# A sandwich of retention and feed-forward: the flag of an early branch, and the last block's closing steps

## The chip, the cores and the metric

The kernel runs on one core of a Trainium2 chip. The metric is the device time of one execution in microseconds (us); a run's result is the median of several executions. Beside these times there is one execution taken by the hardware profiler, from which the page, its views and the trace come.

## The reference, cut to what matters

x has 4 sequences of 1024 tokens with 512 features, in f32. Two residual layers follow each other, each between two layer norms:

```python
x = x + _layernorm(_L0_attn_ref(_layernorm(x), Wq, Wv, Wo, Wg, gamma, lnb, beta))
x = x + _layernorm(_L0_ffn_ref(_layernorm(x), gate_w, up_w, down_w, gate_s, up_s, down_s))
```

The first is a retention: q and v are projected, v runs through a decaying scan along the tokens, the product with q is normalised, gated by silu(x @ Wg.T) and projected by Wo. The second is a feed-forward layer of 1536 hidden units, silu(gate) * up and then down. Its three weights go through float8_e4m3fn before they are used. For weights beyond the range of that format the kernel has a second program, described below.

## The kernel before, in words

**Blocks.** The 4096 tokens are worked in 8 blocks of 512 (`NB` = 8, `TB` = 512), each in 4 tiles of 128 tokens (`NS` = 4). The main loop (line 1214) runs over blocks t; within a block it runs over 12 steps i (`NI` = 12), one for each 128 of the hidden units. A step multiplies gate and up for these units (8 matmuls of 128x512 each), fuses them, and adds an earlier step's product into the four sums of down (2 matmuls for each of the 4 tiles). Between these stands the retention of block t + 1 (`b`), the start of block t + 2 (`n`), and the closing norm of block t - 1 (`l`). Blocks 6 and 7 have fewer such guests, and block 7 (the last, `f.last`) has no retention beside it.

**Order.** The order of the work is written out by hand. Every operation goes through the helper at line 67 (`InOrder`), which keeps it in program order on its engine; that is why nearly all rows of the profile name line 75. All DMAs of the middle of the kernel are issued by SyncE (SP), in this one order too, so a DMA that waits holds those behind it. The weights of the retention come through a ring of four buffers (`w_ring`, `fetch_weights`, line 429): a pass of TensorE that is done releases the load that is four passes ahead.

**Step and lag.** In step i, `fuse(i)` (line 935) takes up's sum times its scale times the gate on VectorE (DVE), ScalarE (ACT) casts it into the upper half of a pair, and `rest(i)` (line 946) forms the lower half on DVE. `down(i)` (line 953) multiplies both halves. It is put `lag` steps behind (line 918): 2 in most blocks, 4 in the last, which has room for seven pairs.

**The tail.** Behind the loop `lag` + 1 steps of down are left (line 1495). They are ordered by tile, so that tile 0's sum closes first: all steps of tile 0 but the last and two of tile 1, then tile 0's last step, then the rest of tile 1, then tiles 2 and 3. Then, for each tile s, DVE multiplies by the scale of down (`scale`) and takes the statistics, ACT takes the root of the variance, DVE adds tile s - 1 to its residual and SP stores it, DVE takes the reciprocal, and the tile is normed: by ACT (`shift_scale`, line 238) for tiles 0 to 2, by DVE (`center_scale`, line 235) for tile 3. Tile 3 is added in two halves (`add_halves`, line 1015); SP stores the first half and ACT the second.

**Flag and branch.** While the weights are rounded, each piece leaves in `over` what tells whether it held a value beyond the format. `pass_over` (line 200) turns that into one number in three parts: DVE sums it and SP writes it as a column to DRAM; SP reads the column back as a row; DVE takes its maximum and SP writes it to DRAM as `flag`. The parts run in steps 2, 3 and 4 of block 7 (line 1373). Behind the last matmul of the program's order, every engine loads `flag` into a register (line 1508), gives a branch hint (line 1514) and later reaches the branch (line 1569). If the flag is zero, it is taken to a short closing piece of code, behind the code of the second program, which rounds the weights exactly and does everything again. There SP waits for its eight DMA semaphores in turn, and then all engines meet at a barrier (line 1615).

Of the kernel before, what the change touches and what calls it, by code (L numbers as in the profile page):

```python
# [15 lines left out]
ALU = mybir.AluOpType  # L16

P = 128
# [5 lines left out]
def sandwich(  # L24
# [20 lines left out]
    nc = tc.nc  # L45
# [4 lines left out]
    TB = 512  # L50
    NS = TB // P
    NB = NT // TB
# [14 lines left out]
    class InOrder:  # L67


        def __init__(self, engine):  # L70
            self.engine = engine
# [5 lines left out]
    pe, dve, act, pool, sp = (  # L77
        InOrder(e) for e in (nc.tensor, nc.vector, nc.scalar, nc.gpsimd, nc.sync)
    )
# [116 lines left out]
    def rounds(n):  # L196
        for _ in range(n):
            next(rounding, None)
# [710 lines left out]
    class Ffn:  # L909
# [3 lines left out]
        def __init__(self, a):  # L913
            self.t, self.kept = a.t, a.kept
            self.parts = [a.x1nT[:, 0], a.x1nT[:, 1]]
            self.f, self.g = {}, {}
            self.last = self.t == NB - 1
            self.lag = 4 if self.last else 2
            self.x1, self.d = [], [None] * NS
            if self.last:  # L920
                self.more = [
                    big.tile([P, 2, 2, TB], F32R, tag=tag, name=f"more_{tag}") for tag in ("xnT", "y")
                ]
# [83 lines left out]
            center(self.d[s], self.d[s], self.mv[:, s, :])  # L1007

        def add(self, s, engine=pool):
            if engine is dve and s == NS - 1:  # L1010
                return self.add_halves(s)
            engine.tensor_tensor(self.d[s], self.d[s], self.x1[s], ALU.add)
            self.store(s)

        def add_halves(self, s):
            for h, queue in enumerate((sp, act)):
                cols = ts(h, D // 2)
                dve.tensor_tensor(self.d[s][:, cols], self.d[s][:, cols], self.x1[s][:, cols], ALU.add)
                queue.dma_start(out[ds(self.t * TB + s * P, P), cols], self.d[s][:, cols])

        def store(self, s):
            sp.dma_start(out[ds(self.t * TB + s * P, P), :], self.d[s])
# [24 lines left out]
    early, later = slice(0, TB // Q // 2), slice(TB // Q // 2, TB // Q)  # L1047
# [162 lines left out]
    splitter.store(7)  # L1210
    rounds(3)

    l = None
    for t in range(NB):
        f, n = Ffn(a), None
        fast = b is not None and b.fast
        for i in range(NI):
# [104 lines left out]
            if t == 0 and i == 9:  # L1322
                load = b.move_x1n(2)
# [10 lines left out]
            if fast and i == 9:  # L1334
                b.o_moments(2)
                loads = [b.move_x1n(s) for s in range(2)]
# [32 lines left out]
            if fast and i == 7:  # L1369
                b.rest_of_y()  # L1370
            splitter.at(t, i, "mid")
            if t == NB - 1 and 1 < i < 5:
                next(passing, None)
            if n and t and i == 2:
                l.fetch(0, 2)
# [115 lines left out]
        l, a, b = f, b, n  # L1491
# [11 lines left out]
    for s in range(2, NS):  # L1503
        for i in steps:
            l.down(i, [s])
    beyond = None
    if flag is not None:
        loads, (beyond,) = nc.values_load_multi_w_load_instructions(
            flag, min_val=0, max_val=0x7F800000,
            skip_runtime_bounds_check_because="it is compared with zero alone",  # L1510
        )
        for load in loads:
            tc.keep_in_program_order(load)
        tc.mark_branch_hint_location("beyond", beyond, engines=mybir.ALL_ENGINES)
    for s in range(NS):
        l.scale(s)
        l.stats(s)
        l.root(s)
        if s:
            l.add(s - 1, dve)  # L1520
        l.inverse(s)
        l.norm(s, shift_scale if s < NS - 1 else center_scale)
    l.add(NS - 1, dve)
    return beyond


# [33 lines left out]
@with_exitstack  # L1560
def retention_ffn_sandwich(ctx: ExitStack, tc: tile.TileContext, *args):


    nc = tc.nc
    out, seq = args[-2:]
    kept = ctx.enter_context(tc.tile_pool(name="flag", bufs=1, space=bass.MemoryType.DRAM))
    flag = kept.tile([1, 1], I32, tag="flag", name="flag")
    beyond = sandwich(tc, *args, flag=flag)
    with tc.If(beyond == 0, preferred_fallthrough_block=False, label="beyond") as within:
        pass  # L1570
    with within.Else():
        with tc.tile_pool(name="rounded", bufs=1, space=bass.MemoryType.DRAM) as kept_rounded:
            weights = round_exactly(tc, kept_rounded, args[8:11], ("gate_w8", "up_w8", "down_w8"))
            sandwich(tc, *args[:8], *weights, *args[11:])
# [44 lines left out]
```

## Time and profile before

| what | us |
|---|---|
| median of three runs (904.69 to 905.27) | 905.08 |
| the profiled execution | 904.03 |
| its span, from the first to the last instruction | 902.2 |
| TensorE busy in the span | 881.1 (98%) |
| DVE busy | 629.8 (70%) |
| ACT busy | 419.0 (46%) |
| POOL busy | 238.9 (26%) |
| mean granted TensorE clock | 0.997 |
| DMA of code: q8, 33 packets | 0.54 MB |
| DMA of code: q14, 37 packets | 0.30 MB |

PE stands for TensorE's matmuls, PEld for its weight loads, POOL for GpSimd. A small q behind an engine's name (SPq, ACTq) means its queue of instructions that are not counted as busy, such as issues of DMAs, branches and waits. In a row of a timeline come the start, the duration, the engine, the line, the operation, what it writes and reads, and in brackets how long the engine had been idle before and what ended that. Rows of equal instructions are merged ("x8"). `pd` are the sums of down, `pfg` and `pfu` those of gate and up, `d` the last norm's tiles, `mvd` their mean and variance, `fuse`, `more_xnT` and `more_y` the pairs. In the rows of a source line come the durations of its instructions (least, median and most, in ns) and the start of the first and last. The page's DMA queues q8 and q14 have the kind "instruction": they load code, in packets of 16 KB (q8) and 8 KB (q14). The end of the span, 1.83 us before the end of the execution's time, is the barrier.

### The profile page before, as it was taken

The numbers are of one execution on the slowest core, as the hardware profiler recorded it, in microseconds if no ns is written. First come the engines' busy times: TensorE is split into PE (matmuls) and PEld (weight loads), VectorE is DVE, ScalarE is ACT, GpSimd is POOL, SyncE is SP. The second block draws the span as 40 slices with busy tenths as digits, with TensorE's granted clock in tenths as the row PEclk, the third lists the DMA queues.
The fourth block names the chain that finished last, engine by engine and source line by source line (L and its number), as shares of the span: only waits on it lengthen the run. The fifth ranks groups of instructions, "written<-read, shape, count | busy, mean of one in ns | idle before, by whom it ended". The sixth has DMA issues, their size and how long they took to land. (4 is left out here: it accounts for less than half of the span.)

```text
span 902.2 us, 12010 instructions
## 1 busy us (share of the span) xinstructions
PE 881.1 (98%) x3948; PEld 738.6 (82%) x3948; DVE 629.8 (70%) x1071; ACT 419.0 (46%) x741; POOL 238.9 (26%) x304
## 2 busy tenths in 40 slices
PE   9999999889999999999999999999999999999995
PEld 7465777678888888888888888888888888888885
DVE  4898788677587766876668675876758756665545
ACT  1358566533645336453464435553364523644323
POOL 1215212201415024230423214141232403322020
PEclk9999999999999999999999999999999999999998
DMA  9974444767563674646754766728746565424021
GB/s 284 304 217 157 151 171 157 205 234 237 171 176 96 232 237 136 153 153 204 250 149 97 232 205 193 187 58 258 226 148 152 154 197 149 152 73 117 0 94 50
DMA packets 116154, 153.73 MB, mean 170 GB/s; under 512 B 10931, under 2 KB 54708, under 8 KB 116020
## 3 DMA queue, kind: packets, MB, share of 16 engines
q1 hardware_dynamic: 115220, 152.23, 55.1%
q8 instruction: 33, 0.54, 0.2%
q10 hardware_dynamic: 864, 0.66, 0.2%
q14 instruction: 37, 0.30, 0.1%
HBM read 117.98 MB, written 39.06 MB: 174 GB/s over the span
## 5 line engine op out<-in xcount | busy, mean ns | idle before, releaser
L75 PE MATMUL pfg<-x1nT,gate_sb 128*128 128x512 f32 x768 | 182.8, 381 | 3.3 <-ACT gate L75 3.2
L75 PE MATMUL pfu<-x1nT,up_sb 128*128 128x512 f32 x768 | 183.2, 381 | 0.8 <-DVE gate L75 0.8
L75 PE MATMUL pd<-down_sb,fuse 128*128 128x512 f32 x720 | 170.5, 379 | 0.0
L75 PEld LDWEIGHTS pfg<-x1nT,gate_sb 128*128 128x128 f32 x768 | 144.2, 189 | 26.7 <-ACT gate L75 6.2
L75 PEld LDWEIGHTS pfu<-x1nT,up_sb 128*128 128x128 f32 x768 | 145.0, 189 | 23.6 <-issue 1.7
L75 PEld LDWEIGHTS pd<-down_sb,fuse 128*128 128x128 f32 x720 | 141.4, 197 | 14.5
L75 DVE SCALAR_TENSOR_TENSOR gate<-pfu,us_sb,gate 128x512 f32<-128x512 f32 x96 | 71.8, 747 | 67.0 <-PE pfu L75 54.8
L75 ACT CAST fuse<-gate 128x512 fp32r<-128x512 f32 x90 | 55.6, 617 | 126.9 <-DVE gate L75 125.2
L75 ACT ACTIVATE gate<-pfg,gs_sb 128x512 f32<-128x512 f32 x96 | 65.6, 683 | 95.5 <-PE pfg L75 95.4
L75 POOL TENSOR_SCALAR mv<-mv 128x1 f32<-128x1 f32 (+1 forms) x82 | 22.8, 278 | 315.0 <-DVE mv L75 312.9
L75 DVE TENSOR_TENSOR fuse<-gate,fuse 128x512 fp32r<-128x512 f32 x90 | 71.7, 797 | 7.4 <-ACT fuse L75 7.3
L75 POOL TENSOR_TENSOR d<-d,x 128x512 f32<-128x512 f32 x28 | 41.7, 1510 | 84.5 <-ACT d L75 70.6
L75 DVE BATCH_NORM_STATS2 st<-x 128x6 f32<-128x512 f32 x64 | 43.6, 681 | 15.2 <-POOL x L75 12.5
L75 POOL TENSOR_TENSOR mv<-mv,nhalf 128x1 f32<-128x1 f32 (+1 forms) x75 | 51.8, 691 | 6.2
L75 POOL TENSOR_TENSOR x<-x,x1n 128x512 f32<-128x512 f32 x32 | 44.7, 1403 | 23.4 <-ACT x1n L75 15.0
L75 ACT ACTIVATE pv<-pv 128x512 f32<-128x512 f32 x28 | 16.3, 581 | 52.9 <-PE pv L75 52.9
L75 POOL TENSOR_TENSOR sqsum<-sqsum,sq 128x512 f32<-128x512 f32 x24 | 33.6, 1401 | 16.0 <-ACT sq L75 8.7
L75 POOL TENSOR_TENSOR ysum<-y 128x512 f32<-128x512 f32 x8 | 10.2, 1275 | 104.2 <-DVE y L75 104.2
L75 DVE TENSOR_TENSOR y<-pq,y 128x512 f32<-128x512 f32 x28 | 19.1, 682 | 22.5 <-PE pq L75 22.5
L75 DVE SCALAR_TENSOR_TENSOR y<-y,lnb_sb,mids 128x512 f32<-128x512 f32 x28 | 27.0, 965 | 7.1 <-ACT mids L75 7.0
L75 ACT ACT_TABLE_LOAD x19 | 24.4, 1283 | 15.5 <-DVE var L75 11.1
L75 DVE BATCH_NORM_STATS2 st<-po 128x6 f32<-128x512 f32 x32 | 21.9, 683 | 13.4 <-PE po L75 13.4
(222 smaller groups left out, 1482.8 us busy)
## 6 DMA issues: line engine op xcount, KB each, us to landing
x<-in_x SPq DMA_DIRECT2D x52, 256.0 KB, 5.6
kept<-x SPq DMA_DIRECT2D x32, 256.0 KB, 2.9
x<-kept SPq DMA_DIRECT2D x32, 256.0 KB, 4.4
out<-d SPq DMA_DIRECT2D x31, 256.0 KB, 2.0
w_ring<-dtop_v SPq DMA_DIRECT2D x24, 256.0 KB, 4.1
w_ring<-dlow_v SPq DMA_DIRECT2D x24, 256.0 KB, 3.2
w_ring<-ddiff_v SPq DMA_DIRECT2D x24, 256.0 KB, 3.6
w_ring<-dtop_q SPq DMA_DIRECT2D x24, 256.0 KB, 2.6
```

The source lines that it names most:

```text
L75: return lambda *args, **kwargs: tc.keep_in_program_order(op(*args, **kwargs))
```

## The change

Four things change. `pass_over` runs in steps 0, 1 and 2 of block 3. ACT, SP and POOL load the flag and give their hint in step 5 of block 6; they load it once more at the old place, for the branch, without a hint. DVE and PE load and hint at the old place. The last block's lag becomes 5. And the last tile is centred by DVE (`center`) behind the add of tile 2 and ahead of the reciprocal, in place of `center_scale` behind it; its two halves are then multiplied by the reciprocal root and added to the residual in one operation each (`spread`).

```diff
-            self.lag = 4 if self.last else 2
+            self.lag = 5 if self.last else 2
...
-            if engine is dve and s == NS - 1:
-                return self.add_halves(s)
...
-        def add_halves(self, s):
+        def center(self, s):
+            dve.tensor_scalar(self.d[s], self.d[s], self.mv[:, s, 0:1], None, ALU.subtract)
+
+        def spread(self, s):
+
             for h, queue in enumerate((sp, act)):
                 cols = ts(h, D // 2)
-                dve.tensor_tensor(self.d[s][:, cols], self.d[s][:, cols], self.x1[s][:, cols], ALU.add)
-                queue.dma_start(out[ds(self.t * TB + s * P, P), cols], self.d[s][:, cols])
+                d = self.d[s][:, cols]
+                dve.scalar_tensor_tensor(
+                    d, d, self.mv[:, s, 1:2], self.x1[s][:, cols], ALU.mult, ALU.add
+                )
+                queue.dma_start(out[ds(self.t * TB + s * P, P), cols], d)
...
+    late = [mybir.EngineType.DVE, mybir.EngineType.PE]
+    early = [mybir.EngineType.Activation, mybir.EngineType.SP, mybir.EngineType.Pool]
+
+    def load_flag(engines):
+        loads, (value,) = nc.values_load_multi_w_load_instructions(
+            flag, engines, min_val=0, max_val=0x7F800000,
+            skip_runtime_bounds_check_because="it is compared with zero alone",
+        )
+        for load in loads:
+            tc.keep_in_program_order(load)
+        return value
+
+    def hint(value, engines):
+
+        tc.mark_branch_hint_location("beyond", value, engines=engines)
...
-            if t == NB - 1 and 1 < i < 5:
+            if flag is not None and t == NB - 2 and i == 5:
+                hint(load_flag(early), early)
+            if t == 3 and i < 3:
                 next(passing, None)
...
-        tc.mark_branch_hint_location("beyond", beyond, engines=mybir.ALL_ENGINES)
+        hint(beyond, late)
+    final = NS - 1
     for s in range(NS):
         l.scale(s)
         l.stats(s)
         l.root(s)
         if s:
             l.add(s - 1, dve)
+        if s == final:
+            l.center(s)
         l.inverse(s)
-        l.norm(s, shift_scale if s < NS - 1 else center_scale)
-    l.add(NS - 1, dve)
+        if s < final:
+            l.norm(s, shift_scale)
+    l.spread(final)
     return beyond
```

## The prediction, as put on record before the changed kernel was run

> **What bounds the kernel now.** I read the page's shares first, then busy time by stretch, then the chain that ended last, and last the end of the run by engine. The page puts PE at 98% of a 902.2 us span, and in the stretches 434 to 540 and 828 to 892.7 us it is busy for 105.98 of 106.00 and 64.59 of 64.70 us. No matmul goes away here, so up to 892.65 us (the last matmul row below, 891.62 + 1.03) the change can only lose time. What can be won lies in the 9.5 us behind it. The chain view shows who holds that stretch (start, duration, what):
>
> ```profile
> 893.73 0.60 DVE d L75
> ...
> 894.36 0.70 DVE st L75
> ...
> 895.97 0.56 DVE d L75
> ...
> 896.89 0.42 DVE d L75
> ```
>
> DVE's chain ends at 897.31, with 4.9 us of span still to come. The timelines of PE and DVE tell why DVE ends so late (start, duration, work, idle before it in brackets):
>
> ```profile
> 882.12 1.89 PE L75 MATMUL pfu<-x1nT,up_sb 128*128 128x512 f32 x8
> ...
> 886.44 0.59 PE L75 MATMUL pd<-down_sb,more_xnT 128*128 128x512 f32 x2
> ...
> 891.62 1.03 PE L75 MATMUL pd<-down_sb,more_xnT 128*128 128x512 f32 x4
> ```
>
> ```profile
> 887.13 0.69 DVE L75 TENSOR_TENSOR d<-pd,ds_sb 128x512 f32<-128x512 f32 x1 [0.87 <-PE pd L75]
> ...
> 889.24 0.69 DVE L75 TENSOR_TENSOR d<-pd,ds_sb 128x512 f32<-128x512 f32 x1
> ...
> 893.65 0.67 DVE L75 TENSOR_TENSOR d<-pd,ds_sb 128x512 f32<-128x512 f32 x1
> ```
>
> DVE waits for PE only ahead of tile 0. From there its own 2.2 us a tile set the pace, and it takes up tile 3 at 893.65, a whole 1.0 us after PE has finished it. The rows of the branch line tell of the last 4.9 us (SP's branch starts at 897.4, the eight waits behind it run from 900.3 to 900.8):
>
> ```profile
> L1569 DVEq COMPARE_BRANCH  x1: 84/84/84, 896.6 to 896.6; - x1
> L1569 DVEq EVENT_SEMAPHORE  x1: 21/21/21, 897.3 to 897.3; - x1
> L1569 SPq COMPARE_BRANCH  x1: 70/70/70, 897.4 to 897.4; - x1
> L1569 ACTq COMPARE_BRANCH  x1: 68/68/68, 897.7 to 897.7; - x1
> L1569 ACTq EVENT_SEMAPHORE  x1: 17/17/17, 900.4 to 900.4; - x1
> ```
>
> ```profile
> SPq L1569 <- SPq L1569: 2.8, 1, 2.8
> ```
>
> SP and ACT stand 2.8 and 2.6 us behind their branches, waiting for nothing but themselves; DVE does not: its next instruction comes 0.7 us later, when its last add (to 897.31) is done. The DMA view shows code loads in this time: one on q14 from 890 to 897 us and three from 897 to 900. So DVE's branch target was there in time, SP's and ACT's were not, though all three had been hinted (SP at 869.6, ACT at 885.6, DVE at 886.4). Counted over the trace, an 8 KB code load follows every 128th instruction of an engine; the last such one falls on ACT at 803.6 us, on SP at 819.3, on DVE at 894.4. Only on DVE does it lie between hint and branch. And no q14 load falls into 880 to 890, when ACT and DVE were hinted. I take from this that a hint loads nothing itself: it turns the next code load.
>
> **The lag of five.** It moves one step of down, 4 tiles of 2 matmuls, from ahead of the last up to behind it: 8 matmuls, 1.73 us (882.12 to 883.85). The last up ends 1.73 us earlier; ahead of tile 0's closing pair now stand 5 steps of tile 0 and 2 of tile 1, 14 matmuls where there were 12, +0.43. The pair moves from 886.44 to 885.14, and DVE's first multiply from 887.13 to 885.83 (-1.30). The last rest, which ended at 886.25, comes 1.73 earlier too, to 884.52, ahead of the 885.14. With DVE's spacing as it is (2.11, 2.22, 2.19) tiles 1 to 3 could start at 887.94, 890.16 and 892.35. PE allows: tiles 2 and 3 now take 12 matmuls each, 2.59 us, so tile 3 is done at 892.65 as before, tile 2 at 890.06, tile 1 at 887.47; with the 0.10 us between PE's end and DVE's start that is 890.16 for tile 2 and 892.75 for tile 3. So tile 3 starts at 892.75, not 893.65: **-0.90**. What is late next is PE itself, which nothing here moves. Step 4 of block 7 loses its down and lasts 3.45 us, like steps 1 to 3 (pfg rows 3.45 apart); DVE's work there is a fuse of 0.75, a rest of 0.69 and two statistics of 0.84, 3.1 us. It fits, the more so as DVE no longer waits 3.43 us for the flag's row at 848.6. Uncovered, each 0.1 us would cost PE 0.1 us.
>
> **The centred last tile.** Before, tile 3 takes 893.65 to 897.31, 3.66 us. The order is then: multiply 0.71, statistics 0.73, aggregate 0.09, add of tile 2 0.60, centre 0.47 (0.55 less the 0.08 by which DVE's rows overlap), reciprocal 0.19, two half spreads. The root (895.30 to 895.60) was covered by the add of tile 2 already, so the centring has no idle time to fill. No half of such a form is in the trace: below it lies the half add (0.34 to the next, 0.42 for the last), above it the whole 512 columns (0.67 and 0.75). I take 0.42 and 0.50: the 0.75 of a whole one less the 0.25 that separates a whole add from a half one. Sum 3.71: **+0.05** (bounds -0.11 and +0.55). So ACT's issue of the last half moves from 897.34 to 896.49.
>
> **The hints.** The last half lands 2.7 us after its issue, so at 900.04 now. SP's eight waits are 0.07 us apart and the landing of ACT's half is the fifth, passed at 900.3 + 4 x 0.07 = 900.58: the branch costs 0.54 us beyond the landing, not 2.8. With the target in place SP passes it as it lands: **-0.54**. In the new program ACT's hint stands 123 instructions ahead of the branch, SP's 58; by their neighbours in the trace that is about 782.5 and 787 us, ahead of the code loads at 803.6 and 819.3. By one rule it saves nothing: the Trainium skill, page "Runtime: NRT & Kernel Launch", section "Instruction fetch mechanics", calls prefetch "purely sequential", so that every taken far branch stalls. DVE's 0.7 us speaks against it; by the rule the change would end at -0.85 and not at the sum below.
>
> **What pays for it.** The loads of the flag move to block 6. ACT's (0.64, with the hint 0.79 to the next instruction) falls behind the two norms of tiles 2 and 3, into 0.94 us of idle ahead of 783.42: nothing. Without that cover pg's scaling would be late by what is over, and PE, which reads it at 784.95, has 0.95 us more. SP's load (1.46 at 868.1) sends three ring loads and the four loads of x from 785.84 to about 787.4; x is first read at 803.56 by POOL, the ring's pieces at 798.0 by PE: nothing. POOL's (0.66) falls into 14.8 us of idle. All three load it again at the end, for the branch: ACT ahead of its table load as before, which is done 2 us ahead of the first root.
>
> The flag in block 3: DVE's reduce and two scalars, 0.57 us, fall into 3.56 us of idle ahead of 415.20; its reduce of the row, 0.27, into the 1.61 ahead of 436.19. SP issues the column (0.32) at about 412.9, where it waits for PE until 415.12. The row must wait until the column has landed, 6.8 us in the trace, 419.7; SP comes to it at 423.2. The flag's own DMA waits for DVE until about 434.9, and behind it stand two loads of kept x (0.90), then a ring load due at 436.12: some 0.1 to 0.3 us late, and PE is four passes away. I take 0, bounds 0 and +0.3, since PE already waits 0.3 us for ACT in this stretch.
>
> **Sum**: -0.90 + 0.05 - 0.54 = -1.39 us. The profiled execution took 904.03 us (1.83 around its span); it would take 902.64. The runs shown have a median of 905.08, 1.05 above it, so I forecast 905.08 - 1.39 = **903.7 us**, or -0.15%. About 0.2%, 1.8 us, is what a measurement of this kernel can tell from no change.
>
> **Rivals.**
> 1. The hints do nothing: too far ahead of their branches, or the loaded code is lost by then. For: no hint in the trace is over 28 us ahead of its branch, and that one (SP's) failed. Against: the count of code loads. SP's branch moves with the last issue, -0.85, and stalls as before: 904.2.
> 2. The landing shortens too. The last halves take 2.5 and 2.7 us, other stores 2.0 in the median, and three code loads run among their packets; SP's and ACT's have moved away to block 6. For: 0.7 us of difference. Against: an engine that enters the target may load what follows it. Price -0.4 to -0.7 on top: 903.0 to 903.3.
> 3. DVE, not PE, keeps the pace and the half spreads cost the upper bound: -0.90 + 0.55 - 0.54, 904.2; with ACT's norms late as well, 904.6.
> 4. Slower: the row in block 3 holds SP's queue. The column's 6.8 us are of an idle DMA system; here 1 MB of x and the ring run beside it. SP's next ring load is due at 425.48, and that piece is read at 431.33, 2.6 us being its usual landing. From a landing over 15.8 us after issue, PE waits one for one; over 19 us the whole is slower than 0.2%, 907 and more. For: 128 pieces of 4 bytes. Against: more than double the measured time is needed.
>
> **How the numbers follow.** Forecast (903.3 to 904.2) 0.57, rival 1 0.12, rival 2 0.15, rival 3 0.08, rival 4 0.08. Faster by over 0.2% (under 903.3): rival 2 and the lower edge of the forecast, 0.24. Slower: rival 4, 0.08. Within: 0.68. The range runs from 902.7 (rival 2, and 0.3 us by which runs differ) to 904.9 (rival 3, likewise); outside lie rival 4 and the tails, 0.18.
>
> **What would show it.** DVE's multiply of tile 0 near 885.8, of tile 3 at 892.75, each behind PE; its last row ending near 896.5; SP's waits at the branch line starting within 0.3 us of its branch; q14 loads from 897 to 900 fewer by two; PE's busy time in 400 to 450 unchanged. Wrong would be: SP's 2.8 us still there, tile 3 at 893.2 or later, or PE idle by over 0.5 us behind 410 us.

## The result, and the profile after

The changed kernel takes 907.17 us (median of 22 runs, 905.23 to 909.83) against 905.57 us for the kernel before, measured beside it (22 runs, 904.28 to 906.98). The ratio is 1.0019, interval 1.0013 to 1.0025: it is slower by 1.7 us (1.2 to 2.3), where 903.7 us, 1.4 under the median then known, were forecast. The profiled execution took 907.53 us with a span of 905.7 us, against 904.03 and 902.2 before.

What was meant to become shorter did. The end of the run by engine, kernel after (start, duration, engine, work, idle before it in brackets; first PE's last row, then rows of DVE):

```profile
896.97 1.03 PE L75 MATMUL pd<-down_sb,more_xnT 128*128 128x512 f32 x4
```

```profile
898.10 0.69 DVE L75 TENSOR_TENSOR d<-pd,ds_sb 128x512 f32<-128x512 f32 x1 [0.29 <-issue]
...
900.24 0.48 DVE L75 TENSOR_SCALAR d<-d,mvd 128x512 f32<-128x512 f32 x1
...
900.83 0.88 DVE L75 SCALAR_TENSOR_TENSOR d<-d,mvd,x 128x256 f32<-128x256 f32 x2
```

PE ends at 898.00, DVE takes up tile 3 at 898.10 and ends at 901.71. The span ends 7.7 us behind PE; before it was 9.5 us. The rows of the branch line, kernel after:

```profile
L1590 SPq EVENT_SEMAPHORE  x8: 17/17/17, 902.3 to 904.4; - x8
...
L1590 SPq COMPARE_BRANCH  x1: 70/70/70, 901.7 to 901.7; - x1
...
L1590 ACTq COMPARE_BRANCH  x1: 68/68/68, 902.1 to 902.1; - x1
L1590 ACTq EVENT_SEMAPHORE  x1: 17/17/17, 902.6 to 902.6; - x1
```

SP's first wait now comes 0.6 us behind its branch and ACT's 0.5 us (2.8 and 2.6 before); SP's fourth and fifth waits now end when the last stores land, where before all eight ran through once the code was there.

So the tail won 1.8 us, and PE lost more: its last matmul starts 5.36 us later than before. Laid matmul by matmul over the trace of before, PE is 1.13 us late at matmul 1700 (408 us) and 5.20 us late at matmul 1800. That is 4.07 us in one place in block 3, where `pass_over` now starts. The chain that ended last runs through it (start, duration, what; kernel after):

```profile
413.62 1.73 PE pd L75 x8
...
416.25 8.02 DMA w_ring<-dtop_q
...
424.40 3.65 PE pq L75 x8
```

In the kernel before no such wait stands in this stretch; the chain leaves PE here for one DMA, a load of the ring that takes 8.02 us. The same load took 2.55 us before. It was issued 2.2 us behind the flag's column, and the loads issued behind the column are late (DMA issues of 412.6 to 419 us, size and time to landing, kernel before and then after):

```profile
w_ring<-dtop_q SPq DMA_DIRECT2D x1, 256.0 KB, 2.5
```

```profile
w_ring<-dtop_q SPq DMA_DIRECT2D x1, 256.0 KB, 8.0
...
w_ring<-ddiff_q SPq DMA_DIRECT2D x1, 256.0 KB, 8.1
beyond<-total SPq DMA_DIRECT2D x1, 0.5 KB, 8.0
```

PE is idle for 2.15 us there, which puts its next matmul 2.3 us behind its due time, and 4.07 are lost. The rest is in the last chain row shown: 8 matmuls in 3.65 us, which take 1.73 elsewhere. The stretches behind the wait tell why (stretch, length, busy time of PE, PEld, DVE, ACT and POOL, granted clock, DMA share, GB/s):

```profile
422.00:424.00 2.00, 0.26 (x2) 0.00 (x0) 1.93 (x4) 0.00 (x0) 1.48 (x4) 1.00 0.42 103
424.00:426.00 2.00, 1.59 (x4) 1.35 (x5) 0.02 (x1) 0.62 (x1) 0.00 (x0) 0.62 0.83 311
426.00:428.00 2.00, 2.00 (x6) 1.53 (x6) 0.00 (x0) 0.00 (x0) 0.00 (x0) 0.53 0.22 66
428.00:430.00 2.00, 2.00 (x11) 1.81 (x10) 0.52 (x1) 1.85 (x3) 0.00 (x0) 1.00 0.55 188
```

PE came back at about half its clock, and had the whole clock again only from 428 us: 3.4 us at half cost the other 1.8 us. Whether all runs paid this second part is not shown. With it the account is +4.07 - 1.79 = +2.3 us, without it about +0.5; the runs say +1.7. The remaining 1.3 us of the offset (5.36 - 4.07) lie at places that none of the changed parts touches, most of it at 197 us, where PE waits for an earlier load of the ring (PE's waits from 186 to 830 us, kernel before and then after):

```profile
PE pv L75 <- DMA w_ring<-dtop_v: 0.2, 1, 0.2
```

```profile
PE pv L75 <- DMA w_ring<-dtop_v: 1.6, 1, 1.6
```

Laid over the trace of before in the same way, the ten kernels below lose between 0 and 1.1 us at this place, whatever their change. That is a difference of executions and is left out of the account.

### The profile page after: what moved, and what is told of

Its sections match the earlier page's. It is cut to its first block, busy times and chain, and to the rows that moved or that the text cites. A ratio compares the mean times of both kernels' runs of the same rounds, so it can differ in the third digit from the quotient of the medians.

```text
span 905.7 us, 12009 instructions
## 1 busy us (share of the span) xinstructions
PE 884.0 (98%) x3948; PEld 740.5 (82%) x3948; DVE 628.9 (69%) x1071; ACT 419.4 (46%) x741; POOL 238.9 (26%) x304
## 4 chain that ended last, share of the span: by engine, by line
PE 79%; DVE 5%; DMA 4%; ACT 2%; issue 1%; SPq 1%; POOL 0%; ACTq 0%; DVEq 0%; POOLq 0%
PE pfu L75 16%; PE pfg L75 16%; PE pd L75 16%; PE pq L75 8%; PE po L75 7%; PE pg L75 7%; PE pv L75 6%; DVE y L75 1%; DMA w_ring<-dtop_q 1%; DMA w_ring<-dtop_v 1%; SPq L75 1%; DVE st L75 1%; DMA xnT<-mx 1%; PE mu L75 0%; DVE x1nT L75 0%
```

## The experiments

Three theories stood at first. Theory Q: the column of 4-byte pieces holds up the loads behind it in SP's queue. Rival E: the pieces hold the DMA engines, whichever queue a load comes from. Rival S: not the column, but DVE's work or the flag's row at the new place. All ratios are to the kernel before, run beside each kernel on the same chip; a ratio of 1.0010 is 0.9 us. "Load behind" is the ring load `w_ring<-dtop_q` issued next behind the added transfer.

| kernel | ratio | interval | load behind, us | PE's wait for the ring near 422 us |
|---|---|---|---|---|
| after | 1.0019 | 1.0013 to 1.0025 | 8.0 | 2.1 |
| e1: tail only, flag and hints at the old place | 1.0006 | 0.9997 to 1.0015 | | none |
| e2: column issued by ACT | 1.0018 | 1.0009 to 1.0027 | 8.6 | 2.5 |
| e3: column behind step 7 of block 3 | 0.9983 | 0.9972 to 0.9994 | | none |
| e4: before, and a column of 128 x 4 bytes written | 1.0033 | 1.0021 to 1.0044 | 8.0 | 2.1 |
| e5: before, and 128 rows of 512 bytes written | 1.0004 | 0.9995 to 1.0013 | 2.6 | none |
| e6: before, with the new hints, flag as in e3 | 0.9989 | 0.9980 to 0.9998 | | none |
| e7: before, and 32 x 4 bytes written | 1.0011 | 1.0002 to 1.0019 | 6.5 | 0.6 |
| e8: before, and 128 x 4 bytes read | 0.9999 | 0.9990 to 1.0008 | 2.6 | none |
| e9: after, column widened to 512-byte rows | 0.9979 | 0.9970 to 0.9988 | 2.6 | none |
| e10: e3 without the centring | 0.9977 | 0.9968 to 0.9986 | | none |

**e4, the column alone.**

```diff
+            if flag is not None and (t, i) == (3, 0):
+                aside = dram.tile([P, 1], F32, tag="aside", name="aside", bufs=1)
+                sp.dma_start(aside, eps_sb)
             if t == NB - 1 and 1 < i < 5:
                 next(passing, None)
```

> The kernel before, with one more write and nothing else: a column of 128 pieces of 4 bytes of a constant goes to DRAM on SP's queue in step 0 of block 3, at the place where the change issues the flag's column. Its own flag stays in block 7. Theory Q and rival E: the loads behind it land in 6 to 8.5 us and PE waits for dtop_q and the next two, 4.1 us in sum; 905.6 + 4.1 = 909.7. Rival S: nothing but one issue of 0.32 us that SP makes while it waits; 905.6.

PE's longest wait from 186 to 830 us, kernel e4 (who waited for what: us, times, longest):

```profile
PE pq L75 <- DMA w_ring<-dtop_q: 2.1, 1, 2.1
```

The kernel before with 512 bytes more to write, and nothing else, has the whole stall: 3.0 us (1.9 to 4.0). S falls: DVE's part of the flag, the row and the flag's own store are not needed for it.

**e2, another queue.**

```diff
-        sp.dma_start(column, bits)
+        act.dma_start(column, bits)
```

> The changed kernel, with one DMA put on another queue: ACT issues the column in block 3, SP all else as in the change. Theory Q: the loads of dtop_q, dlow_q and ddiff_q land in 2.5 to 3.5 us, not 8; PE loses nothing in block 3; the time is 1.8 us under before, 903.8. Rival E (the pieces hold up the engines whatever the queue): they land in 6 to 8 us and the time stays at 907.2. Rival S (DVE's work or the row): 907.2 as well, with loads that land in 2.5 to 3.5 us.

Kernel e2, the column in the DMA issues and PE's longest wait:

```profile
beyond<-total ACTq DMA_DIRECT2D x1, 0.5 KB, 8.4
```

```profile
PE pv L75 <- DMA w_ring<-ddiff_v: 2.5, 1, 2.5
```

PE now waits one pass earlier, for a ring load that SP had issued 0.15 us ahead of ACT's column. Loads in another queue, and even one issued sooner, are held. Q falls and E stands. The Trainium skill, page "DMA: Bandwidth & Descriptors", section "Issuing engines are not separate DMA queues", says that DMAs of all issuing engines run on the same 16 DMA engines and interleave there; this run agrees, and its price is in the row above.

**e5, e8 and e7: what in the column holds the engines.** Three variants of e4's transfer at e4's place:

```diff
 e5: aside is [P, P]
+                sp.dma_start(aside, ident)
 e8: aside is a tile in SBUF
+                sp.dma_start(aside, x[0:1, 0:P].rearrange("o p -> p o"))
 e7: a quarter of the column
+                sp.dma_start(aside[:P // 4], eps_sb[:P // 4])
```

> Kernel before with one more store at the place of the moved column: 128 rows of 512 bytes (64 KB) instead of 128 pieces of 4 bytes. Theory E (the 4-byte pieces hold up the DMA engines, for every queue): the three ring loads behind it land in 2.5 to 3.5 us, PE has no wait for the ring, the time is that of before (within 0.4 us). Rival (any store at this place, or the added issue on SP, delays the ring): the same 3 us as with the column, ring loads at 6 to 8 us, PE waits about 2 us.

> Kernel before with 128 pieces of 4 bytes read from memory into a column of 128 partitions at the place of the moved column, nothing written to memory. If the pieces hold up the engines whichever way they go, the ring loads land in 6 to 8 us and the time is about 3 us longer. If only writes of 4 bytes to memory do, the ring loads take 2.5 to 3.5 us and the time is that of before.

> Kernel before with a column of 32 pieces of 4 bytes in the place of the moved column, a quarter of it. If the delay is a time for each piece (the ring loads landed about 5.3 us later than usual behind 128 pieces), it is about 1.3 us here; the ring's piece has 3.3 us to spare ahead of PE, so PE does not wait and the time is that of before. If it is a fixed time for any transfer of such pieces, the ring loads take 8 us as with 128, PE waits about 2 us, the time is 3 us longer.

The DMA issues of 412.6 to 419 us, in e5, e8 and e7 in this order:

```profile
w_ring<-dtop_q SPq DMA_DIRECT2D x1, 256.0 KB, 2.6
...
aside<-ident SPq DMA_DIRECT2D x1, 64.0 KB, 3.2
```

```profile
w_ring<-dtop_q SPq DMA_DIRECT2D x1, 256.0 KB, 2.6
...
aside<-in_x SPq DMA_DIRECT2D x1, 0.5 KB, 2.9
```

```profile
w_ring<-dtop_q SPq DMA_DIRECT2D x1, 256.0 KB, 6.5
...
aside<-eps_sb SPq DMA_DIRECT2D x1, 0.1 KB, 6.3
```

A write of 128 times as many bytes, in rows of 512, holds nobody, and neither do 128 pieces of 4 bytes that are read. What holds the engines is writing 4-byte pieces to memory. The packets in the traces agree. Between 412 and 426 us, 14 to 21 packets of 2 KB take over 1 us in the four kernels that write such pieces there, the longest 5.0 us in after, 4.9 in e2, 4.7 in e4 and 3.7 in e7. In the eight others none takes over 0.92 us; the median packet of data takes 0.08 us in all twelve. No run tells whether it matters that the pieces lie side by side in one stretch of 512 bytes, since every column written was of this kind. For e7 neither expectation was right: a quarter of the pieces gives not a quarter of the delay (1.3 us) and not all of it, but 6.5 - 2.6 = 3.9 us where 128 pieces give 8.0 - 2.6 = 5.4. By these two points most of the delay is there with the first 32 pieces. PE's wait then is 0.6 us, no halved clock follows it, and the kernel loses 1.0 us (0.2 to 1.7). PE's wait in e7:

```profile
PE pq L75 <- DMA w_ring<-dtop_q: 0.6, 1, 0.6
```

**e9, the changed kernel without 4-byte writes.** The flag stays in steps 0 to 2 of block 3.

```diff
-        column = dram.tile([P, 1], I32, tag="beyond", name="beyond", bufs=1)
-        sp.dma_start(column, bits)
+        wide = work.tile([P, TB], I32, tag="ret", name="wide")[:, :P]
+        dve.tensor_copy(wide, bits.to_broadcast([P, P]))
+        column = dram.tile([P, P], I32, tag="beyond", name="beyond", bufs=1)
+        sp.dma_start(column, wide)
...
-        sp.dma_start(row, column.rearrange("p o -> o p"))
+        sp.dma_start(row, column[:, 0:1].rearrange("p o -> o p"))
```

> The changed kernel, its flag still at steps 0 to 2 of block 3, but the flag's column is widened: DVE copies it to 128 columns (one copy of 128x128 more), 128 rows of 512 bytes are written, and the row is read as 128 pieces of 4 bytes out of them. Theory (only 4-byte writes hold the engines): ring loads land in 2.5 to 3.5 us, PE has no wait on the ring and no halved clock behind it, the tail stays 7.5 to 7.8 us behind PE; time 1.0 to 2.0 us under before, 904.0 to 905.0. Rival (the flag's place in block 3 costs by itself, by DVE's work, SP's order or the row): PE waits near 424 us as in the changed kernel, time at or above before.

The same place in PE's timeline, kernel e9:

```profile
419.27 1.89 PE L75 MATMUL pfu<-x1nT,up_sb 128*128 128x512 f32 x8
421.00 1.03 PE L75 MATMUL pq<-xnT,w_ring 128*128 128x512 f32 x4
421.86 1.03 PE L75 MATMUL pq<-low,w_ring 128*128 128x512 f32 x4
```

No wait and the full clock; the column lands in 3.4 us. The extra copy takes 0.23 us, in DVE's idle time. This version is faster than both kernels, by 1.9 us (1.1 to 2.7) against the one before, and its profiled execution ends 7.5 us behind PE. The prediction's other terms for block 3 (DVE's scalars, the row, the flag's own store) come out at nothing here: against the kernel before PE loses nothing from 410 to 430 us, and the 0.46 us that it then loses near 435 us, waiting for ACT, are 0.42 in e3 and 0.35 in e5, which have no part of the flag there.

**e3, another place.** The parts of `pass_over` run at the steps below, so that the column is issued at 481.5 us, where PE has no load of the ring close ahead.

```diff
-            if t == 3 and i < 3:
+            if (t, i) in ((3, 7), (4, 1), (4, 2)):
```

> The changed kernel with the three parts of the flag at other steps: the column in step 7 of block 3, where SP's next DMA is due some 10 us later, the row in step 1 and the flag in step 2 of block 4. Theory Q and rival E: nothing waits behind the column; PE loses nothing; 903.8. Rival S: the row and DVE's work stand in the same steps of block 4 as in block 3 of the change, so PE waits there, 2 to 4 us; 906 to 907.

No stall, and 1.5 us under before (0.5 to 2.5). The row is issued only at 530.8, which nobody minds.

**e1, the tail alone.** The lag and the centring of the changed kernel, with the flag back in block 7 and all loads and hints of it at the old place.

```diff
-            if flag is not None and t == NB - 2 and i == 5:
-                hint(load_flag(early), early)
-            if t == 3 and i < 3:
+            if t == NB - 1 and 1 < i < 5:
                 next(passing, None)
...
-        hint(beyond, late)
+        hint(beyond, late + early)
```

> The change with its lag of five and its centred last tile alone: flag, loads and hints stand where they stood before. Theory Q (the column of 4-byte pieces holds up the ring loads that follow it in SP's queue): PE does not stand still behind 410 us, its last matmul ends as before, the tail is 0.95 us shorter (tile 3 taken up 0.90 earlier, 0.05 less behind it), SP and ACT still stand 2.6 to 2.9 us behind their branches; 904.6 against a before of 905.6. Rival S (it is not the column but the DVE work and the row of the moved flag) and rival E (4-byte pieces hold up the DMA engines for every queue) expect the same here; had the lag itself lost time in block 7, PE's last matmul would end later and the time be 905.6 or more.

Missed by about 1.5 us (+0.5 us measured, -0.3 to +1.4, where -0.95 was expected), and the trace shows where most of it went: behind 836 us PE and DVE wait (kernel e1, waits of 836 to 900 and of 836 to 870 us):

```profile
PE pfu L75 <- DVE gate L75: 0.9, 1, 0.9
```

```profile
DVE total L75 <- DMA row<-beyond: 3.8, 1, 3.8
```

DVE waited for the flag's row in block 7 in the kernel before too (3.4 us), and PE did not feel it. With the lag of five, one step of down has gone from this stretch, and PE reaches up's next sum before DVE has emptied it: its next matmul starts 1.05 us late, after 0.9 us of idle. The tail itself does what it should, the span ends 8.4 us behind PE. So the lag needs the flag out of block 7: two parts of the change that look independent are not.

**e6, the hints alone**, with lag and ending as before and the flag as in e3.

```diff
...
+            if flag is not None and t == NB - 2 and i == 5:
+                hint(load_flag(early), early)
-            if t == NB - 1 and 1 < i < 5:
+            if (t, i) in ((3, 7), (4, 1), (4, 2)):
                 next(passing, None)
...
-        tc.mark_branch_hint_location("beyond", beyond, engines=mybir.ALL_ENGINES)
+        beyond = load_flag(late + early)
+        hint(beyond, late)
```

> Kernel before with the flag made in blocks 3 and 4 (column behind step 7 of block 3, as in the run at which the stall was gone) and the hints of ScalarE and SyncE in block 6; the lag of four and the two half adds of the old tail are kept. Theory: the two hints alone are worth what SP and ACT no longer wait behind their branches, -0.5 to -0.9 us, and SP's eight waits start within 0.7 us of its branch; time 0.5 to 0.9 us under before. Rival (the hints gain only together with the earlier end of the last tile): no difference to before, SP still 2.8 us behind its branch.

The branch line in kernel e6:

```profile
L1582 SPq EVENT_SEMAPHORE  x8: 17/17/17, 899.1 to 901.1; - x8
...
L1582 SPq COMPARE_BRANCH  x1: 70/70/70, 898.5 to 898.5; - x1
```

0.6 us behind its branch SP waits, and the span ends 8.7 us behind PE where it was 9.5: without lag and centring the hints and the moved flag are worth 0.8 us of tail, and 1.0 us (0.2 to 1.8) of time.

**e10, the ending.** e3 with the old ending of the last tile.

```diff
-        if s == final:
-            l.center(s)
         l.inverse(s)
-        if s < final:
-            l.norm(s, shift_scale)
-    l.spread(final)
+        l.norm(s, shift_scale if s < final else center_scale)
+    l.add_halves(final)
```

> The changed kernel with the column behind step 7 of block 3 and with the old ending of the last tile (centre and scale in one pass, then two half adds) in place of the centring during the root and two half spreads. Expected from the rows: from the start of the last tile's multiply to DVE's last end 3.66 us instead of 3.61 to 3.64, so up to 0.05 us longer than with the centring, within what can be told from no change; the time about 1.5 us under before. If the centring were worth what the earlier end of DVE is (-0.95), the tail would be 8.4 to 8.6 us behind PE and not 7.5 to 7.8.

Rows of DVE's last tile in kernel e10:

```profile
893.92 0.69 DVE L75 TENSOR_TENSOR d<-pd,ds_sb 128x512 f32<-128x512 f32 x1 [0.29 <-issue]
...
896.84 0.76 DVE L75 TENSOR_TENSOR d<-d,x 128x256 f32<-128x256 f32 x2
```

From take-up to end 893.92 to 897.60, 3.68 us, where after and e9 need 3.61 with the centring. The end of the span came 8.0 us behind PE, above the 7.5 to 7.8 expected, because the last store landed 2.5 us behind its issue here and 2.1 to 2.4 in after, e3 and e9. The time cannot be told from that of e3 or e9.

## Why the prediction was wrong

**The step that failed** is "The flag in block 3 ... I take 0, bounds 0 and +0.3". It measured 4.07 us in the profiled execution (by the ratios of after and e9 about 3.6), and its cause was no row on the list. The step asked where each part of the flag waits and who stands behind it in SP's queue. It did not ask what the column does to the transfers beside it. The sign was in the trace of before: 512 bytes took 6.8 us to land on DMA engines with nothing else to do, while 256 KB took 2.5 to 3. The flag's column (DMA issues of 840 to 850 us), and in block 3 the matmuls that read the ring load of the first section, kernel before:

```profile
beyond<-total SPq DMA_DIRECT2D x1, 0.5 KB, 6.8
```

```profile
420.97 1.03 PE L75 MATMUL pq<-xnT,w_ring 128*128 128x512 f32 x4
```

I read the 6.8 us as a latency; e4, e5 and e8 show that it is a time for which loads beside it are held as well. In block 7 no load of the ring was near, so it cost nothing there. In block 3 the piece that PE reads at 420.97 landed at 417.67 in before, 3.3 us early; a delay of 5.5 us (8.02 - 2.55) uses these up and leaves 2.2, the wait that the profile shows.

**Rival 4** named the right block, the right 4-byte pieces and a time of "907 and more", and the wrong mechanism. It let the column land late and the row hold SP's queue, from a landing over 15.8 us. The column landed in 8.0 us, the row was issued at 428.46, 6.4 us behind that landing, and SP was never held by it. It was given 0.08 because by that mechanism the measured 6.8 us would have had to double; by the real one they did not have to grow at all.

**The clock** was in no term. "PE waits one for one" is true of the first 2.3 us alone; the halved clock behind them added another 1.8.

**The lag of five**: right. DVE takes up tile 3 0.10 us behind PE's end as forecast (-0.90), and tile 0 after 1.30 us of idle. Step 4 of block 7 "fits, the more so as DVE no longer waits 3.43 us for the flag's row": right, and e1 shows that without this it costs 1.05 us.

**The centred last tile**: forecast +0.05, measured -0.07 (3.61 against e10's 3.68). The two half spreads take 0.88 us together, against the 0.42 and 0.50 taken for them, and the centring 0.40 to the next start instead of 0.47.

**The hints**: forecast -0.54. In e6 SP passes the wait for the last half 0.02 us behind its landing, where in before it was 0.57: -0.55, right. So a hint 110 us (SP) and 116 us (ACT) ahead of its branch works, and rival 1 falls. That it "turns the next code load" agrees with the count of code loads on q14 from 894 us on: six in before and in e1, which hints at the old place, four in after and in e6. The rule of the Trainium skill's page "Runtime: NRT & Kernel Launch", section "Instruction fetch mechanics" ("purely sequential") does not hold for hinted branches here: with the target not next in sequence, SP and ACT were stopped for 0.6 and 0.5 us instead of 2.8 and 2.6.

**Rival 2** (the landing shortens too): the last store took 2.7 us in before and 2.4 in after and e6, which with the 0.12 us of the centring is why the tail won 1.79 us and not 1.39. But with the hints at the old place it took 2.5 in e1, and with the new ones 2.1 in e9 and 2.5 in e10. That the code loads set it is not shown; why it varies stays open. Rival 3 falls, since DVE waits for PE ahead of tiles 0 and 3.

**The signs** that were named. Less PE's 5.36 us, tile 0 is taken up at 885.83 and tile 3 at 892.74, and DVE's last row ends at 896.35: as forecast, like the code loads, fewer by two. SP's waits start 0.5 us behind its branch, not within 0.3. And "PE idle by over 0.5 us behind 410 us", named as what would be wrong, came.

**The sum** mended: tail -1.79, block 3 +4.07 with the halved clock or about +2.3 without; +0.5 to +2.3 us in all, where +1.7 was measured. With block 3 at the forecast's zero, e9 shows what the rest is worth: -1.9 us.

## What to carry to other kernels

Before a small transfer is moved, ask what it does to the transfers beside it, not only who waits for it: a landing time far above that of a transfer hundreds of times its size is a warning. Where one number per partition must go to memory beside urgent loads, write whole rows of 512 bytes and read the column back out of them. And test the parts of a change that share an engine together: the longer lag was only free because another part had taken a wait off DVE.

## What the runs showed of the hardware

- 128 pieces of 4 bytes written to memory held back 256 KB loads by 5.4 us (after, e4) to 6.0 us (e2), from SP's queue and from ACT's alike, a load issued just ahead of them included; 32 pieces from SP's queue by 3.9 us. The same pieces read, and 128 rows of 512 bytes written, held back nothing (2.6 us). The Trainium skill, page "DMA: Bandwidth & Descriptors", section "Specifications", names 512 bytes as the least transfer for line rate, with a read-modify-write below it. The three runs agree with such a bound for writes and not for reads; that a read-modify-write is what happens was not tested, and rows between 4 and 512 bytes were not tried.
- PE's granted clock fell to a half for 3.4 us behind waits of 2.1 to 2.5 us (after, e2, e4), and did not behind the 0.6 us of e7 or the 0.9 us of e1. The Trainium skill, page "TensorE: Matmul & The Clock Gate", Part 1, puts the fall behind an idle window of about 3.4 us; here it came behind shorter waits. Nor does length alone decide: the wait of 2.29 us near 181 us was followed by 8 matmuls in 1.99 us in before and in 2.92 us in after; of all twelve kernels four (after, e1, e9 and e10) show the halved clock there. It cost after nothing in the end, since PE in before stood still for 1.5 us a little later, waiting for DVE, and in after it did not: at 190 us after is 0.1 us late. Two rows of PE's timeline, before and then after:

```profile
181.07 1.99 PE L75 MATMUL pfg<-x1nT,gate_sb 128*128 128x512 f32 x8 [2.29 <-ACT gate L75]
```

```profile
181.20 2.92 PE L75 MATMUL pfg<-x1nT,gate_sb 128*128 128x512 f32 x8 [2.29 <-ACT gate L75]
```
